# A two-layer graph network on one core: the attention steps of a group moved eleven slots ahead in a written-out plan, one copy behind another reader, two bias copies on another engine

## The chip, the cores and the metric

One Trainium2 chip, one core of it. The metric is the device time of the kernel in microseconds, as the median of several runs. All tensors are float32.

## The reference

128 graphs of 128 nodes with 256 features. Layer 0 is a graph convolution, layer 1 a graph attention with eight heads; both are preceded by a layer norm with a ReLU, and both add their input.

```
h   = relu(layernorm(x));   x1 = x + adj @ (h @ w0) + b0
h2  = relu(layernorm(x1))
feat_proj = (h2 @ fc_w + fc_b) split in 8 heads
logits = q + k^T                          # q, k: one number for each node and head
masked = leaky_relu(logits + (1 - adj) * -1e9, 0.01)
attn   = softmax(masked);   out = attn @ feat_proj
y = sigmoid(concat(out) @ fp_w + fp_b + h2);   result = x1 + y
```

## The kernel before

**Groups and units.** Four graphs make a group, so there are 32 groups, numbered from 0. The main loop has one period for each group. In a period TensorE does the attention products of its group in four units (two halves of the heads, two pairs of heads in each): it aggregates the features with the attention (`aggregate`, line 614) and multiplies the result by the folded weights of the heads (`multiply`, line 661). `take` (line 632) carries each aggregate out of PSUM: five tensors are copied or subtracted on ScalarE, VectorE and GpSimd (f0, f3, f4, f1 are ScalarE copies; f5 = g - f0 is a VectorE subtraction that reads the same PSUM bank as f4; f6 and f2 are GpSimd subtractions). Each aggregate takes one of four PSUM banks in turn, shared with the products of layer 0 and with q and k.

**Slots.** A unit has eleven steps, the list `ORDER`, so a period has 44 slots. In each slot TensorE gets four 128x256 products' worth of work (an `aggregate`, or a `multiply` of the unit before), and then the steps that `PLAN` has for this slot are issued. A plan entry is (slot, who, function, arguments): `who` says which group the step works on, counted from the group of the period (1 is the next group), and "u" means the units themselves. The order of the text is the order on each engine: nothing is rescheduled, each engine and the one DMA queue in use (SyncE's, called SP) runs its own instructions strictly in this order, and waits where an operand is not there.

**What a group goes through before its period.** Layer 0 of group g+3 (`n1_apply`, `first_a`, `first_b`, `n2_stats`) runs in slots 25 to 41 of period g; ScalarE copies `ahT` for `first_a` in slot 35, TensorE needs them for `first_b` in slots 37 and 40. `n2_apply`, `leave_h2` and `fetch_h2` (slots 3 to 5) make h2 of group g+2 and pass it through device memory for a blockwise transpose; `turn_h2_blocks`, `make_qk`, `turn_qk`, `load_k` (slots 18, 24, 28, 34) make q and k of group g+2, k again through device memory (`k_mem`, then `kq`). The attention of group g+1 then fills slots 0 to 33 of period g, graph by graph:

- `masked` (line 523) on VectorE: a transposing spread of `kq` into 128x1024 (L518), and the mask added (L526)
- `leaky` (line 536) on ScalarE: eight instructions, one for a head (L539)
- `head_max` (L547) on VectorE, `exps` on ScalarE (L555), eight for a graph
- `normal` (line 560): a reciprocal on VectorE (L563), and a product on GpSimd (L564)
- `leave_attention` and `fetch_attention` for each pair of graphs: 1 MB to device memory (`a_mem`, L431) and back in four transfers (`attnB`, L575); the second waits for the first in the SP queue
- `turn` (line 586): a blockwise transpose on VectorE (L588), in four parts: pair 0 and 1 of the first half of the heads in slots 34 and 40, pair 0 and 1 of the second half in slots 12 and 13 of the next period

**What follows a period.** `combine` (line 695) of the group before, in slots 6 and 11: ScalarE copies an accumulator with the bias to `p1` (L718), VectorE adds (L704), and the accumulators in PSUM (one set, `acc0` and `acc1`) are free for the new group, which first writes them in slots 12 and 18. Then `leave_z`, `fetch_z`, `turn_z`, `residual` (GpSimd), `sigmoid` (ScalarE, slot 28), `finish` (VectorE, slot 29), `store`. `begin` and `load_blocks` (slot 8) load the inputs of later groups on the same SP queue: `xg`, `ag`, and four transfers `agB`.

Periods 0, 1 and 31 have plans of their own. `EARLIER`, `ATTENTION` and `QK` exist only in the changed kernel.

Of the kernel before, what the change touches and what calls it, by code (L numbers as in the profile page):

```python
# [10 lines left out]
AF = mybir.ActivationFunctionType  # L11
ALU = mybir.AluOpType
# [16 lines left out]
def gnn_then_gat_kernel(  # L29
# [16 lines left out]
    nc = tc.nc  # L46
    NG = x.shape[0] // GB
# [40 lines left out]
    fpb_o = const.tile([P, NC], FP, name="fpb_o")  # L88
# [525 lines left out]
    def aggregate(u, b, c):  # L614
        s = u["s"]
        g = u["g", b, c] = bank([P, HU * P], "g_ps")
        w = HU * P // len(u["pairs"])
        for n, pair in enumerate(u["pairs"]):
            lhsT = (
                s["hs"][:, pair]  # L620
                if c == 2
                else s["h2"][:, 2 * pair + b].rearrange("p j c q -> p (j c q)")[:, ts(c, P)]
            )
            nc.tensor.matmul(  # L624
                g[:, n * w : (n + 1) * w],
                lhsT=lhsT,
                rhs=s["aT", pair, u["half"]][:, b, u["heads"]],
                start=True,
                stop=True,
            )  # L630

    def take(u, b, c):

        g, f = u["g", b, c], u["f"]

        def new(m):
            f[m] = pool["un"].tile([P, HU * P], FP, name=f"f{m}", tag=f"f{m}")
            return f[m]

        if (b, c) == (0, 0):  # L640
            nc.scalar.copy(new(0), g)  # L641
        elif (b, c) == (1, 1):
            nc.scalar.copy(new(3), g)  # L643
        elif (b, c) == (1, 2):
            nc.scalar.copy(new(4), g)  # L645
            nc.vector.tensor_tensor(new(5), g, f[0], ALU.subtract)  # L646
            nc.gpsimd.tensor_tensor(new(6), f[3], f[5], ALU.subtract)  # L647
        else:
            nc.scalar.copy(new(1), g)  # L649
            nc.gpsimd.tensor_tensor(new(2), f[1], f[5], ALU.subtract)  # L650
# [4 lines left out]
    ORDER = [("g", 0, 0), 3, 0, ("g", 1, 1), 1, 4, ("g", 1, 2), 6, 5, ("g", 0, 1), 2]  # L655

    def acc_of(s, part, slots, pairs):
        acc = s["acc", part]
        return acc[:, pairs, slots].rearrange("p a s n -> p s a n") if s["g"] in PAIRWISE else acc[:, slots, pairs]
# [24 lines left out]
    def z_blocks(s, k0, k1, pairs):  # L684

        if s["g"] == NG - 1:
            z = s["zT"].rearrange("p (k a i q) -> p k a i q", k=4, a=2, q=Q)
        else:
            z = s["zT"].rearrange("p (i k a q) -> p k a i q", k=4, a=2, q=Q)
        return z[:, k0:k1, pairs]  # L690

    def blocks(t):
        return t.rearrange("p s a (i q) -> p s a i q", q=Q)

    def combine(u, m):

        s = u["s"]
        pairs = slice(u["pairs"][0], u["pairs"][-1] + 1)  # L700
        n = len(u["pairs"])

        def add(o, a, b):
            nc.vector.tensor_tensor(o, a, b, ALU.add)  # L704

        def acc(part, a, b):
            return acc_of(s, part, slice(a, b), pairs)

        def temp(name, slots):
            return small.tile([P, slots, 2, P], FP, name=name, tag=name, bufs=1)[:, :, 0:n]  # L710

        if m == 4:
            if pairs.start == 0:
                s["zT"] = pool["un"].tile([P, GB * D], FP, name="zT", tag="zT", bufs=1)
            p1 = temp("p1", 2)
            w = s["w"] = temp("w", 2)
            for c in range(NC):
                nc.scalar.activation(  # L718
                    p1[:, c : c + 1], acc(0, 0, 1), AF.Identity, bias=fpb_o[:, c : c + 1]
                )  # L720
            add(w, acc(0, 1, 3), p1)
            add(z_blocks(s, 0, 1, pairs), blocks(acc(0, 3, 4)), blocks(p1[:, 0:1]))
        elif m == 2:
            w = s["w"]
            p6 = temp("p6", 1)
            v = temp("v", 2)
            nc.vector.tensor_copy(p6, acc(1, 0, 1))
            add(v, acc(1, 1, 3), p6.to_broadcast([P, 2, n, P]))
            add(
                z_blocks(s, 2, 4, pairs), blocks(w),  # L730
                blocks(v[:, 0:1]).to_broadcast([P, 2, n, NB, Q]),
            )
            add(z_blocks(s, 1, 2, pairs), blocks(w[:, 1:2]), blocks(v[:, 1:2]))
# [48 lines left out]
    def sigmoid(s, b0, nb):  # L782
        z = s["z"][:, b0 : b0 + nb]
        nc.scalar.activation(z, z, AF.Tanh, scale=0.5)

    def finish(s, b0, nb):
        bs = slice(b0, b0 + nb)
        nc.vector.scalar_tensor_tensor(
            s["z"][:, bs], s["z"][:, bs], 0.5, s["x1"][:, bs], ALU.mult, ALU.add
        )  # L790

    def store(s, b0, nb):
        bs = slice(b0, b0 + nb)
        nc.sync.dma_start(
            out[GB * s["g"] + b0 : GB * s["g"] + b0 + nb].rearrange("b n d -> n b d"),
            s["z"][:, bs],
        )
# [3 lines left out]

    PLAN = [
        (0, "u", take, 0, 0, 0),
        (0, 1, masked, 0),
        (0, 1, masked, 1),
        (0, 1, leaky, 0),
        (3, "u", take, 0, 1, 1),
        (3, 2, n2_apply, 0),
        (3, 2, n2_apply, 1),
        (3, 2, leave_h2),  # L810
# [13 lines left out]
        (13, -1, fetch_z),  # L824
        (11, "u", take, 1, 0, 0),
        (11, 1, leaky, 2),
        (12, 0, turn, 0, 1),
        (12, 1, masked, 3),
        (12, 1, normal, 0),
        (13, 0, turn, 1, 1),  # L830
        (14, "u", take, 1, 1, 1),
        (14, 1, head_max, 2),
        (14, 1, exps, 1, 0, 8),
        (17, "u", take, 1, 1, 2),
        (18, 2, turn_h2_blocks),
        (18, 1, normal, 1),
        (18, 1, leave_attention, 0),
        (20, 1, fetch_attention, 0),
# [6 lines left out]
        (21, -1, residual, 1),  # L845
        (22, "u", take, 2, 0, 0),
        (22, 1, exps, 3, 0, 4),
        (24, 2, make_qk),
        (25, "u", take, 2, 1, 1),
        (25, 1, normal, 2),  # L850
        (25, 1, exps, 3, 4, 4),
        (25, 3, n1_apply, 0),
        (25, 3, n1_apply, 1),
        (27, "u", combine, 1, 4),
        (28, "u", take, 2, 1, 2),
        (28, 2, turn_qk),
        (28, 1, normal, 3),
        (28, 3, turn_blocks),
        (28, 4, n1_stats, 0),
# [28 lines left out]
    FIRST_PLAN = [  # L888
        (0, "u", take, 0, 0, 0),
        (0, 3, load_blocks),  # L890
        (3, "u", take, 0, 1, 1),
        (3, 0, leaky, 3),
        (3, 0, exps, 2, 0, 4),
        (7, "u", take, 0, 1, 2),
        (7, 0, exps, 2, 4, 4),
        (7, 0, head_max, 3),
# [86 lines left out]
    ]  # L983


    SECOND_PLAN = [step for step in PLAN if step != (5, 1, masked, 2)]
    SECOND_PLAN.insert(SECOND_PLAN.index((6, "u", combine, -1, 4)) + 1, (6, 1, masked, 2))
    for old, new in (((12, 0, turn, 0, 1), (12, 0, turn, 1, 0)),):
        SECOND_PLAN[SECOND_PLAN.index(old)] = new
    LAST_PLAN = [step for step in PLAN if step != (12, 0, turn, 0, 1)]  # L990
    LAST_PLAN.insert(LAST_PLAN.index((5, 1, masked, 2)), (4, 0, turn, 0, 1))
    plans = {0: FIRST_PLAN, 1: SECOND_PLAN, NG - 1: LAST_PLAN}

    groups = [{"g": g} for g in range(NG)]
    pool = {}
# [113 lines left out]
    for g in range(NG):  # L1109
        cur = groups[g]  # L1110
        last = units[-1]
        units = []
        for n in range(4):
            each = g in PAIRWISE
            units.append({
                "s": cur,
                "pairs": (n // 2,) if each else (0, 1),
                "half": n % 2 if each else n // 2,
                "heads": slice(0, HU) if each else slice(n % 2 * 2, n % 2 * 2 + 2),
                "first": n % 2 == 0 if each else n == 0,  # L1120
                "last": n % 2 == 1 if each else n == 3,
                "f": {},
            })
        for slot in range(4 * len(ORDER)):
            n, i = divmod(slot, len(ORDER))
            o = ORDER[i]
            if isinstance(o, tuple):
                aggregate(units[n], o[1], o[2])
            elif n or last:
                multiply(units[n - 1] if n else last, o)  # L1130
            for at_, who, f, *args in plans.get(g, PLAN):
                if at_ != slot:
                    continue
                if who == "u":
                    u = last if args[0] < 0 else units[args[0]]
                    if u and not (f is combine and args[0] > 0 and g not in PAIRWISE):
                        f(u, *args[1:])
                elif g + who in range(NG):
                    f(groups[g + who], *args)
            if g == NG - 1 and slot == 33:  # L1140
                turn_z_by_products(cur, 0)
                sigmoid(cur, 0, 2)
            if g == NG - 1 and slot == 35:
                finish(cur, 0, 2)
                store(cur, 0, 2)
# [42 lines left out]
```

## Time and profile before

| what | value |
|---|---|
| median of 3 runs | 1747.33 us (1746.8 to 1747.98) |
| the profiled execution | 1749.97 us, its span 1748.0 us |
| mean granted TensorE clock | 0.96 |
| ScalarE `exps`, 1024 instructions (L555) | 398.6 us busy |
| ScalarE `leaky`, 1024 instructions (L539) | 313.7 us busy |
| VectorE `masked`, spread and add (L518, L526) | 156.9 and 180.6 us busy |
| moved by DMA | 251.34 MB, 144 GB/s |

A row of the profile names the line of the kernel, the engine, the operation and the tiles (out<-in); "idle before, releaser" tells how long the engine sat idle just before such instructions and what it had waited for. The chain of waits is followed back from the last instruction to what released it. The periods can be read off TensorE's rows: the second pair's product of slot 0 waits for `attnT` in nearly every period, for example at 968.82, 1024.02 and, two periods before the last, at 1602.48 us.

### The profile page before, as it was taken

How to read it: one execution, taken by the hardware profiler on the slowest of the kernel's cores; microseconds unless marked ns; L12 is line 12 of the kernel's file. 1: busy time of each engine (PE TensorE's matmuls, PEld its weight loads, DVE VectorE, ACT ScalarE, POOL GpSimd, SP SyncE). 2: the span in 40 equal slices, each digit the busy share in tenths (PEclk: the TensorE clock that was granted, in tenths of full speed). 3: DMA queues.
4: the chain of work that ended last, by engine and by line, in shares of the span. 5: the costliest groups of instructions: out<-in, count | busy, mean ns of one | idle time of the engine just before them, and what ended most of it. 6: DMA issues, size and time to landing. Idle time of an engine off the chain costs nothing.

```text
span 1748.0 us, 24792 instructions
## 1 busy us (share of the span) xinstructions
PE 1539.2 (88%) x7661; PEld 1291.6 (74%) x7661; DVE 1174.1 (67%) x1816; ACT 1194.6 (68%) x4045; POOL 917.4 (52%) x845
## 2 busy tenths in 40 slices
PE   7789898989888899888989888989888998988898
PEld 6567777777777777777777777777777877777686
DVE  6667676667676666676667676667676667675654
ACT  4778766668766668766668766678766678666662
POOL 6646454556454555445555445555445655445453
PEclk9999999999999999999999999999999999999999
DMA  4136555565555465555565545564554565554441
GB/s 162 27 93 184 144 155 136 148 171 156 148 153 152 136 170 156 148 135 156 147 173 146 156 130 144 158 183 137 148 147 139 161 177 144 142 139 130 140 133 48
DMA packets 281760, 251.34 MB, mean 144 GB/s; under 512 B 155398, under 2 KB 237724, under 8 KB 273436
## 3 DMA queue, kind: packets, MB, share of 16 engines
q1 hardware_dynamic: 281628, 249.77, 51.5%
q8 instruction: 60, 0.98, 0.3%
q14 instruction: 72, 0.59, 0.1%
HBM read 135.93 MB, written 113.77 MB: 143 GB/s over the span
## 4 chain that ended last, share of the span: by engine, by line
ACT 47%; DMA 18%; DVE 14%; PE 9%; issue 6%; POOL 5%; SPq 2%; DVEq 0%; POOLq 0%; ACTq 0%
ACT attn L555 17%; ACT attn L539 14%; DMA attnB<-a_mem 9%; DMA a_mem<-attn 7%; ACT h L326 6%; PE acc L676 5%; POOL attn L564 4%; DVE attn L526 3%; DVE attn L518 3%; PE g_ps L624 3%; DVE attnT L588 2%; ACT f L649 2%; ACT f L643 2%; SPq L575 2%; ACT f L645 2%
## 5 line engine op out<-in xcount | busy, mean ns | idle before, releaser
L676 PE MATMUL acc<-f,wts 128*128 128x256 f32 (+1 forms) x3920 | 914.5, 375 | 69.5 <-DVE zT L704 69.5
L676 PEld LDWEIGHTS acc<-f,wts 128*128 128x128 f32 x3920 | 726.2, 199 | 194.3 <-ACT f L649 76.2
L624 PE MATMUL g_ps<-attnT,h 128*128 128x256 f32 (+1 forms) x1464 | 419.9, 405 | 74.6 <-DVE attnT L588 71.9
L555 ACT ACTIVATE attn<-attn,nmax 128x128 f32<-128x128 f32 x1024 | 398.6, 405 | 0.0
L647 POOL TENSOR_TENSOR f<-f,f 128x512 f32<-128x512 f32 x128 | 162.8, 1272 | 407.3 <-DVE f L646 407.3
L624 PEld LDWEIGHTS g_ps<-attnT,h 128*128 128x128 f32 x1464 | 277.1, 196 | 133.7 <-DVE attnT L588 82.0
L539 ACT ACTIVATE attn<-attn,q 128x128 f32<-128x128 f32 x1024 | 313.7, 397 | 85.9 <-DVE attn L526 85.9
L564 POOL TENSOR_TENSOR attn<-attn,total 128x1024 f32<-128x1024 f32 x128 | 249.0, 1946 | 153.2 <-DVE total L563 152.6
L588 DVE STREAM_TRANSPOSE attnT<-attnB 128x1024 f32<-128x1024 f32 x124 | 151.9, 1225 | 170.2 <-DMA attnB<-a_mem 141.0
L646 DVE TENSOR_TENSOR f<-g_ps,f 128x512 f32<-128x512 f32 x128 | 88.1, 688 | 201.9 <-ACT f L645 201.7
L555 ACT ACTIVATION_READ_ACCUMULATOR attn<-attn,nmax 128x1 f32 x1024 | 209.5, 205 | 0.0
L526 DVE TENSOR_TENSOR attn<-attn,mask 128x1024 f32<-128x1024 f32 x128 | 180.6, 1411 | 4.5
L547 DVE TENSOR_REDUCE nmax<-attn 128x8 f32<-128x1024 f32 x128 | 153.9, 1202 | 33.3 <-ACT attn L539 33.2
L650 POOL TENSOR_TENSOR f<-f,f 128x512 f32<-128x512 f32 x128 | 164.7, 1287 | 3.3 <-ACT f L649 3.3
L649 ACT COPY f<-g_ps 128x512 f32<-128x512 f32 x128 | 75.4, 589 | 127.4 <-PE g_ps L624 126.8
L641 ACT COPY f<-g_ps 128x512 f32<-128x512 f32 x128 | 75.1, 587 | 123.0 <-PE g_ps L624 123.0
L518 DVE STREAM_TRANSPOSE attn<-kq 128x1024 f32<-128x1024 f32 x128 | 156.9, 1226 | 2.8 <-DMA kq<-k_mem 2.8
L645 ACT COPY f<-g_ps 128x512 f32<-128x512 f32 x128 | 74.6, 582 | 115.8 <-PE g_ps L624 115.6
L624 PE MATMUL g_ps<-attnT,hs 128*128 128x256 f32 (+1 forms) x488 | 132.5, 392 | 9.0 <-POOL hs L612 9.0
L390 PE MATMUL x_ps<-w_sb,ahT 128*128 128x256 f32 x512 | 120.5, 379 | 0.0
L305 POOL TENSOR_SCALAR rstd<-mv 128x4 f32<-128x4 f32 x61 | 12.7, 225 | 203.8 <-DVE mv L294 203.7
L624 PEld LDWEIGHTS g_ps<-attnT,hs 128*128 128x128 f32 x488 | 92.0, 191 | 22.0 <-POOL hs L612 10.0
(107 smaller groups left out, 1524.3 us busy)
## 6 DMA issues: line engine op xcount, KB each, us to landing
a_mem<-attn SPq DMA_DIRECT2D x62, 1024.0 KB, 3.8
attnB<-a_mem SPq DMA_DIRECT2D x248, 256.0 KB, 4.7
xg<-in_x_dram SPq DMA_DIRECT2D x32, 512.0 KB, 4.2
z_mem<-zT SPq DMA_DIRECT2D x31, 512.0 KB, 2.7
zB<-z_mem SPq DMA_DIRECT2D x124, 128.0 KB, 3.0
out_dram<-z SPq DMA_DIRECT2D x31, 512.0 KB, 4.7
h_mem<-h SPq DMA_DIRECT2D x29, 512.0 KB, 2.8
h2B<-h_mem SPq DMA_DIRECT2D x116, 128.0 KB, 2.9
```

The source lines that it names most:

```text
L390: nc.tensor.matmul(op[:, bb, :], lhsT=s["ahT"][:, 2 * b2 + bb, c, :], rhs=w0_sb[:, c, :], start=(c == 0), stop=(c == NC - 1),)
L518: nc.vector.transpose(s["v", b], s["kq"][:, :, b].unsqueeze(3).to_broadcast([P, NB, H, Q]),)
L526: nc.vector.tensor_tensor(a, a, s["mask"][:, b, :] .rearrange("p (j c) -> p j c", c=Q) .unsqueeze(2) .to_broadcast([P, NB, H, Q]), ALU.add,)
L539: nc.scalar.activation(a[:, :, h, :], a[:, :, h, :], AF.Prelu, bias=s["q"][:, b, h : h + 1], alpha=0.01,)
L547: nc.vector.tensor_reduce(nmax, a.rearrange("p j h c -> p h j c"), AX.XY, ALU.max, negate=True)
L555: nc.scalar.activation(a[:, :, h, :], a[:, :, h, :], AF.Exp, bias=s["nmax", b][:, h : h + 1], accum_out=s["total", b][:, h : h + 1],)
L564: nc.gpsimd.tensor_tensor(a, a, total.unsqueeze(1).unsqueeze(3).to_broadcast([P, NB, H, Q]), ALU.mult)
L588: nc.vector.transpose(attention_tile(s, pair, half).rearrange("p b h (i r) -> p i b h r", r=Q), s["ab", pair][:, :, :, ts(half, HU)],)
L624: nc.tensor.matmul(g[:, n * w : (n + 1) * w], lhsT=lhsT, rhs=s["aT", pair, u["half"]][:, b, u["heads"]], start=True, stop=True,)
L647: nc.gpsimd.tensor_tensor(new(6), f[3], f[5], ALU.subtract)
L650: nc.gpsimd.tensor_tensor(new(2), f[1], f[5], ALU.subtract)
L676: nc.tensor.matmul(acc, lhsT=wt[m][:, u["half"] * HU + h, :], rhs=f[:, n], start=(first and n == 0 and m in ((3, 6) if each else (3, 1, 6, ...
```

## The change

- In `take`, the copy of f4 is issued after the subtraction that makes f5.
- In `combine`, the two copies with the bias (`p1`) go to VectorE.
- In `PLAN`, the two late `turn` entries go from slots 12 and 13 to 2 and 3, and `turn_h2_blocks`, `make_qk` and `turn_qk` go from 18, 24 and 28 to 21, 25 and 29.
- All attention steps and all q and k steps of group 5 and later are then issued eleven slots earlier than `PLAN` says; groups 2, 3 and 4 are 0, 4 and 8 slots earlier. `turn` is not among them. Steps with slots below eleven land in the period before, so slots 33 to 43 of period g now hold the start of the attention of group g+2.
- In each slot, the steps that are not moved are issued first.

```diff
         elif (b, c) == (1, 2):
+            nc.vector.tensor_tensor(new(5), g, f[0], ALU.subtract)
             nc.scalar.copy(new(4), g)
-            nc.vector.tensor_tensor(new(5), g, f[0], ALU.subtract)
...
             for c in range(NC):
-                nc.scalar.activation(
-                    p1[:, c : c + 1], acc(0, 0, 1), AF.Identity, bias=fpb_o[:, c : c + 1]
+                nc.vector.tensor_scalar(
+                    p1[:, c : c + 1], acc(0, 0, 1), fpb_o[:, c : c + 1], None, ALU.add
                 )
...
-        (12, 0, turn, 0, 1),
+        (2, 0, turn, 0, 1),
...
-        (13, 0, turn, 1, 1),
+        (3, 0, turn, 1, 1),
...
-        (18, 2, turn_h2_blocks),
+        (21, 2, turn_h2_blocks),
...
-        (24, 2, make_qk),
+        (25, 2, make_qk),
...
-        (28, 2, turn_qk),
+        (29, 2, turn_qk),
...
+    ATTENTION = (masked, leaky, head_max, exps, normal, leave_attention, fetch_attention)
+    QK = (turn_h2_blocks, make_qk, turn_qk, load_k)
+    EARLIER = {2: 0, 3: 4, 4: 8}
+
+    plans = {g: [] for g in range(NG)}
+    plans[0] = FIRST_PLAN
+    for f_of in (False, True):
+        for g in range(1, NG):
+            for at_, who, f, *args in PLAN:
+                moved = f in ATTENTION or f in QK
+                if moved != f_of:
+                    continue
+                if g == 1 and f is turn and who == 0:
+                    at_ += 10
+                    args = (1, args[0])
+                slot = len(ORDER) * 4 * g + at_
+                if moved:
+                    slot -= EARLIER.get(g + who, 11)
+                period, at_ = divmod(slot, 4 * len(ORDER))
+                who = who if who == "u" else who + g - period
+                plans[period].append((at_, who, f, *args))
```

In a steady period of the changed kernel the SP queue therefore has this order: `leave_h2`, `fetch_h2` (slots 3, 5), `leave_attention` of pair 0 (7), the six loads (8), `fetch_attention` of pair 0 (9), `leave_z`, `fetch_z` (11, 13), `k_mem` (18), `leave_attention` of pair 1 (19), `fetch_attention` of pair 1 (22), the four `kq` (23), `store` (34). Before it was: `leave_h2`, `fetch_h2`, the six loads, `leave_z`, `fetch_z`, pair 0 out (18) and back (20), `k_mem` (28), pair 1 out (30) and back (33), the four `kq` (34), `store`.

More of the change, by code (lines that the diff above doesn't have):

```diff
@@ L983, in gnn_then_gat_kernel @@
     ]
[L986 to L992, printed above, removed]
+    ATTENTION = (masked, leaky, head_max, exps, normal, leave_attention, fetch_attention)
[18 more added lines that the diff above has]
+                plans[period].append((at_, who, f, *args))
     groups = [{"g": g} for g in range(NG)]
@@ L1130, in gnn_then_gat_kernel @@
                 multiply(units[n - 1] if n else last, o)
-            for at_, who, f, *args in plans.get(g, PLAN):
+            for at_, who, f, *args in plans[g]:
                 if at_ != slot:
```

## The prediction

> **What bounds the kernel now.** I read the busy shares first, then the chain of waits, then the waits, the SP queue and TensorE in order of time.
>
> ```profile
> PE 1539.2 (88%) x7661; PEld 1291.6 (74%) x7661; DVE 1174.1 (67%) x1816; ACT 1194.6 (68%) x4045; POOL 917.4 (52%) x845
> ...
> ACT attn L555 17%; ACT attn L539 14%; DMA attnB<-a_mem 9%; DMA a_mem<-attn 7%; ACT h L326 6%; PE acc L676 5%; POOL attn L564 4%; DVE attn L526 3%; DVE attn L518 3%; PE g_ps L624 3%; DVE attnT L588 2%; ACT f L649 2%; ACT f L643 2%; SPq L575 2%; ACT f L645 2%
> ```
>
> No engine is full: TensorE has 88%, but the chain that ends last is the attention of the next group. One turn of it, in order of time (start, duration):
>
> ```profile
> 1007.69 1.93 POOL attn L564
> ...
> 1009.64 5.72 DMA a_mem<-attn
> ...
> 1016.69 5.91 DMA attnB<-a_mem
> ...
> 1022.72 1.25 DVE attnT L588
> 1023.97 0.59 DVE x L397
> ...
> 1025.74 1.25 DVE attn L518
> ```
>
> The last graph's product goes out and back, VectorE turns it (slot 40), and `masked` of the next group (slot 0), behind it in VectorE's queue, starts at once at 1025.74. So the attention is a loop with one turn per period: the spread of graph 0 starts at 970.54 and at 1025.74. TensorE pays for it here:
>
> ```profile
> DVE f L646 <- ACT f L645: 201.7, 65, 6.7
> DVE attnT L588 <- DMA attnB<-a_mem: 141.0, 27, 9.9
> PE g_ps L624 <- DVE attnT L588: 71.9, 30, 7.3
> PE acc L676 <- DVE zT L704: 69.5, 29, 3.2
> ...
> 546.91 0.70 PE L624 MATMUL g_ps<-attnT,h 128*128 128x256 f32 x2 [2.19 <-DVE attnT L588]
> 547.45 3.52 PE L676 MATMUL acc<-f,wts 128*128 128x256 f32 x8
> ```
>
> After such a wait eight products take 3.52 us, not the usual 1.89; the granted clock at 548 to 550 is 0.50. Counting TensorE's rows at full clock (0.864 us a slot, 1.9 for `first_a`, 3.5 for `first_b`, 0.7 for q and k) gives 44.0 us a period; slot 0 of periods 2 and 30 (179.81 and 1653.26) lie 28 turns of 52.6 us apart. The 8.6 us between are these waits and the slow clock after them.
>
> SP has one period like this:
>
> ```profile
> 820.28 0.38 SPq L435 DMA_DIRECT2D h_mem<-h  x1
> ...
> 825.12 0.42 SPq L67 DMA_DIRECT2D xg<-in_x_dram  x1
> ...
> 829.95 0.48 SPq L431 DMA_DIRECT2D z_mem<-zT  x1
> 833.75 1.74 SPq L742 DMA_DIRECT2D zB<-z_mem  x4
> ...
> 850.62 0.34 SPq L431 DMA_DIRECT2D a_mem<-attn  x1
> 854.43 1.74 SPq L575 DMA_DIRECT2D attnB<-a_mem  x4
> 856.27 1.80 SPq L498 DMA_DIRECT2D kq<-k_mem  x4
> ...
> kq<-k_mem SPq DMA_DIRECT2D x128, 16.0 KB, 4.6
> ```
>
> The loads hold SP 4.8 us (825.12 to 829.95), `zB` waits 3.8 us for `z_mem`, `attnB` 3.8 us for `a_mem`, and `kq` stands behind `attnB`.
>
> **What the change removes.** `attnB` comes back far ahead of `turn` in slots 34 and 40, so those waits go (71.9 us on TensorE, most of the slow clock after them). The moved `p1` takes two ScalarE copies, 0.8 us, off the path to `acc0` and puts 0.8 us on VectorE (as L727, 413 ns each). VectorE (36.1 us busy of some 52.4 in windows of a period) and ScalarE (36.7) have room. If nothing else held, a period would be 44 us plus a few small waits.
>
> **What it adds: a new loop.** Slots 33 to 43 now hold `masked`, `leaky`, `head_max` of a group among the last steps of layer 0, and in each queue they stand ahead of these: `leaky` 0 (slot 33) before the `ahT` copies (35) on ScalarE, `finish` before `masked` on VectorE, and `kq` (23) behind pair 1's way out and back on SP. Let 0 be the start of `masked` of graph 0. By rows of before (net spacing when back to back):
> - to the start of `leaky` 0: 2.54 (1025.74 to 1028.28); `leaky` 2.36; first `ahT` copy 0.5: 5.4
> - `first_b`, eight products, which wait for that copy: 1.73 at full clock, 3.2 at half (1654.27, after a wait of 7.3). TensorE will have waited long, so 3.2: 8.6
> - VectorE, strictly in this order: add 0.7, statistics 1.15, `head_max` 0 1.13, `masked` 2 2.45, f5 of slot 39 0.6: 14.6
> - ScalarE: f4 now waits for that f5 (before, f5 waited for f4), and all the rest stands behind it: f4, f1 0.47 each, `exps` 0 3.09, f0 0.47, `leaky` 2 2.36, f3 0.47, `n2_apply` 1.98, `exps` 1 3.09: 27.0
> - VectorE over the same stretch: turn, add, statistics, two maxima, `masked` 3, two turns, `combine` with `p1`, f5 of slot 7: 12.4 too, 27.0
> - GpSimd: f6 1.25, `normal` 1 1.9: 30.2
>
> Now SP may send pair 0 out: 0.35; the six loads, which pass from ahead of it to behind it, 4.9 (4.6 to 5.2 before); pair 0 back 1.75 (the outward way ends meanwhile); `z_mem` to `zB`, 3.7 to 4.8 before, now behind 1 MB of `attnB`: I take 4.9; `zB` 1.75; `k_mem` 0.35; pair 1 out, waited for 3.8; then pair 1 back and `kq`, whose last issue is 3.3 us after the first `attnB` and lands 4.6 later: 7.9. Sum 25.7. `normal` 3 would be ready earlier than SP (at about 40 against 44), so SP sets it. The next `masked` 0 can start at 55.9: **the loop takes 56 us, not 52.6**, and TensorE, with about 47 of work and small waits, idles some 8 us before each `first_b`.
>
> Bounds. The front part is 28.7 if `first_b` runs at full clock, 30.7 if the adds are slowed like the one of 1.96 us at 974.24. `z_mem` behind `attnB` has no row; nearest are a store behind nothing (2.7 to landing) and `out_dram`, a store of the same size that follows `attnB` and `kq` closely (4.0 to 6.2, median 4.7), plus 0.5 to issue; I lean to the second, as its place is alike. `a_mem` takes 3.8, at times 5.7. `kq` lands in 3.8 to 5.9. All the lowest at once give SP 23.4, all the highest 31.0; with one or two of them at their ends it is 24.4 to 28.5, and the loop 53 to 59.
>
> Here the Trainium skill bears, in "DMA: Bandwidth & Descriptors", section "Queues, rings and completion order": each DMA engine takes the descriptors of a queue in ring order. Our two medians for a store (2.7 and 4.7 us) agree. By the rule `z_mem` always pays for `attnB`; without it the loop would be some 2 us shorter.
>
> "TensorE: Matmul & The Clock Gate", section "What's actually happening", says that the clock falls to half after an idle window of about 3.4 us; here a wait of 2.19 was enough once (546.91), and by either an idle of 8 us is paid.
>
> **Sum.** `masked` 0 of group 5 starts at 287.7 before; the ramp can gain up to 15 us, I take 4. There follow 26 turns to group 31. From there 15.6 us to slot 0 of period 30, about 40.5 for period 30 (no layer 0, no q and k left, 50.7 before), and 44.1 from 1703.93 to the end as before: 100. Without the loads the last two turns save 6. Total 378 + 26 x 56 = 1834 against a span of 1748.0. That execution was 2.6 us above the median of runs, its span 0.7 above it; so **1835 us**. Break-even is a loop of 52.7.
>
> **Rivals.**
> - *Faster.* The place is SP, the price of `kq`. If SP reaches pair 1's way out before `normal` 3 is done, the loop is closed by ScalarE alone: about 38.5 to the end of `normal` 3 at full clock (39.1 before), 3.8 out, 7.9 for `kq`, 50.2. Total 378 + 26 x 50.2 = 1683, 65 us faster. It decides from the point where SP's 25.7 falls below 22.4. For it: SP has free stretches before, such as 858.6 to 871.9. Against: all my lowest terms at once give 23.4. If `kq` were early as well, TensorE would set about 47.6, 1616 us. 17%.
> - *No change.* The parts of SP overlap better than I count, and the loop is 52.5 to 52.8. For it: all the lowest bounds, 28.7 and 23.4, give 52.1. Against: they would have to be met nearly all at once, though TensorE's idle time excludes the full clock. 4%.
> - *Much slower.* The 1 MB transfers of pair 0, the loads, `z_mem` and pair 1 are now one burst; if `a_mem` takes 5.7 and `z_mem` 6.5 in each turn, the loop is 59.5, 1925 us. 10%.
> - *Does not do what it says.* f4 behind f5 is free only while VectorE is on time. In slot 39 it is some 5 us late, so ScalarE idles there. Undone, f1 would still wait for TensorE's slot 42 at about 13 to 15, so this is worth 1 us of a turn, 26 us in all, and does not turn the sign.
>
> **How the numbers follow.** The forecast (loop 53.5 to 58.5, 1770 to 1900 us) has 69%, faster 17%, no change 4%, over 1900 us 10%. About 0.2% (3.5 us) is what a measurement can tell. The range of 8 in 10 reaches from 1700, into the faster case, to 1905. Faster 0.17, same 0.04, slower 0.79.
>
> **What would show it.** Right: spreads of graph 0 (L518) 56 us apart; before each an idle VectorE released by `kq<-k_mem`; TensorE waiting for the `ahT` copy 6 to 10 us before `first_b` (L390), clock 0.5 behind it; hardly any wait of `turn` for `attnB`. Wrong: the spread waits for nothing or for `finish`; `kq` issued within 40 us of the spread before; TensorE's waits under 4 us a period. It would be wrong as a whole if SP's stretch from pair 0 out to `kq` is shorter than 22 us.

## The result, and the profile after

The changed kernel takes **1993.22 us** (median of 4 runs, 1992.11 to 2002.91), the kernel before 1747.65 us beside it (4 runs, 1746.8 to 1753.78): 1.1409 times as long, interval 1.1364 to 1.1453. The profiled execution has a span of 1990.4 us and a mean granted clock of 0.90 (0.96 before). It is slower, as forecast, but by 246 us and not by 88, and outside the range of 1700 to 1905 us.

Three lines of its page: the busy shares, the chain that ended last by line, and the landing time of the store `z_mem`, which was 2.7 us before.

```profile
PE 1603.2 (81%) x7661; PEld 1344.7 (68%) x7661; DVE 1169.9 (59%) x1886; ACT 1173.7 (59%) x3975; POOL 940.8 (47%) x845
...
DMA z_mem<-zT 9%; PE acc L676 8%; DMA a_mem<-attn 7%; PE x_ps L390 7%; DMA kq<-k_mem 6%; ACT attn L539 6%; ACT attn L555 6%; SPq L575 4%; PE g_ps L624 4%; DVE attn L518 3%; SPq L77 3%; DVE attn L526 3%; SPq L742 2%; ACT h L326 2%; DVE nmax L547 2%
...
z_mem<-zT SPq DMA_DIRECT2D x31, 512.0 KB, 6.5
```

Before, `exps` and `leaky` on ScalarE led the chain (17% and 14%); both are now at 6%. `z_mem` leads with 9% and `kq` has 6%, and neither is on the line of before; with `a_mem` (7% in both) these are transfers of the SP queue. Between them stand TensorE's products L676 and L390 (`first_b`), with 8% and 7%. Every engine is less busy in share.

One turn of the loop in the changed kernel's timeline (start, duration, and in brackets the idle time before):

```profile
1018.37 1.25 DVE L518 STREAM_TRANSPOSE attn<-kq 128x1024 f32<-128x1024 f32 x1 [3.96 <-DMA kq<-k_mem]
...
1080.62 1.25 DVE L518 STREAM_TRANSPOSE attn<-kq 128x1024 f32<-128x1024 f32 x1 [3.95 <-DMA kq<-k_mem]
...
1085.51 1.04 ACT L381 COPY ahT<-ah_ps 128x512 f32<-128x512 f32 x2
...
1086.12 3.74 PE L390 MATMUL x_ps<-w_sb,ahT 128*128 128x256 f32 x8 [8.19 <-ACT ahT L381]
```

The spread of graph 0 waits for `kq` each time, 62.25 us apart here and 62.0 on the mean of 23 turns (337.36 to 1764.19 us). Behind it come `leaky`, the `ahT` copies, and a TensorE that has stood for 8.19 us and does eight products in 3.74.

SP in the same turn:

```profile
1049.42 0.34 SPq L431 DMA_DIRECT2D a_mem<-attn  x1
...
1056.22 2.88 SPq L575 DMA_DIRECT2D attnB<-a_mem  x4
1059.20 0.38 SPq L431 DMA_DIRECT2D z_mem<-zT  x1
1065.86 1.73 SPq L742 DMA_DIRECT2D zB<-z_mem  x4
1067.68 0.38 SPq L493 DMA_DIRECT2D k_mem<-k  x1
1068.15 0.38 SPq L431 DMA_DIRECT2D a_mem<-attn  x1
1072.40 1.74 SPq L575 DMA_DIRECT2D attnB<-a_mem  x4
1074.24 3.00 SPq L498 DMA_DIRECT2D kq<-k_mem  x4
```

This is the predicted order, from pair 0 out to `kq`, and each step takes longer than the forecast had it: 31.2 us from 1049.42 to the next spread (29.7 to 32.1 in the turns between 337.36 and 1639.89 us). The view by stretches of time (length, busy time of each engine, then granted clock, mean busy share of the 16 DMA engines, and GB/s) for the front part and the two parts of SP's stretch:

```profile
1018.37:1049.42 31.05, 24.23 (x100) 20.36 (x100) 24.24 (x33) 21.78 (x77) 12.26 (x15) 0.84 0.12 32
1049.42:1068.15 18.73, 15.74 (x80) 13.48 (x81) 5.96 (x12) 11.65 (x43) 7.48 (x5) 0.91 0.86 218
1068.15:1080.62 12.47, 8.66 (x47) 7.21 (x45) 5.64 (x13) 2.60 (x4) 9.09 (x8) 1.00 0.86 233
```

In the first half of a turn the DMA engines do almost nothing (0.12, 32 GB/s, 1.0 MB), in the second they are busy at 0.86 and move 7.0 MB (218 x 18.73 + 233 x 12.47). VectorE and ScalarE stand the other way round: 24.24 and 21.78 us of work in the first half, 11.60 and 14.25 in the second. The change has made two halves of a turn out of what ran side by side.

The waits say the same (who waited for what: us in total, times, longest):

```profile
DVE z L749 <- DMA zB<-z_mem: 294.1, 30, 11.8
...
PE x_ps L390 <- ACT ahT L381: 205.1, 27, 8.4
...
DVE attn L518 <- DMA kq<-k_mem: 104.7, 28, 4.3
```

VectorE's wait for `attnB`, 141.0 us before, is down to 5.0.

### The profile page after: what moved, and what is told of

It is laid out like the page before. It is cut to its first block, busy times and chain, and to the rows that moved or that the text cites. A ratio compares the mean times of both kernels' runs of the same rounds, so it can differ in the third digit from the quotient of the medians.

```text
span 1990.4 us, 24642 instructions
## 1 busy us (share of the span) xinstructions
PE 1603.2 (81%) x7661; PEld 1344.7 (68%) x7661; DVE 1169.9 (59%) x1886; ACT 1173.7 (59%) x3975; POOL 940.8 (47%) x845
## 4 chain that ended last, share of the span: by engine, by line
DMA 26%; PE 19%; ACT 17%; DVE 16%; SPq 14%; issue 5%; POOL 3%; DVEq 0%; ACTq 0%; POOLq 0%
DMA z_mem<-zT 9%; PE acc L676 8%; DMA a_mem<-attn 7%; PE x_ps L390 7%; DMA kq<-k_mem 6%; ACT attn L539 6%; ACT attn L555 6%; SPq L575 4%; PE g_ps L624 4%; DVE attn L518 3%; SPq L77 3%; DVE attn L526 3%; SPq L742 2%; ACT h L326 2%; DVE nmax L547 2%
## 5 line engine op out<-in xcount | busy, mean ns | idle before, releaser
L676 PE MATMUL acc<-f,wts 128*128 128x256 f32 (+1 forms) x3920 | 935.9, 380 | 17.0 <-ACT attn L555 7.3
L676 PEld LDWEIGHTS acc<-f,wts 128*128 128x128 f32 x3920 | 734.5, 201 | 150.8 <-ACT attn L555 19.9
L647 POOL TENSOR_TENSOR f<-f,f 128x512 f32<-128x512 f32 x128 | 163.8, 1280 | 558.4 <-DVE f L645 459.9
L624 PE MATMUL g_ps<-attnT,h 128*128 128x256 f32 (+1 forms) x1464 | 401.4, 394 | 22.2 <-ACT f L649 12.8
L390 PE MATMUL x_ps<-w_sb,ahT 128*128 128x256 f32 x512 | 169.4, 490 | 205.1 <-ACT ahT L381 205.1
L646 ACT COPY f<-g_ps 128x512 f32<-128x512 f32 x128 | 74.5, 582 | 377.1 <-DVE f L645 376.9
L390 PEld LDWEIGHTS x_ps<-w_sb,ahT 128*128 128x128 f32 x512 | 123.7, 249 | 238.2 <-ACT ahT L381 216.4
L749 DVE STREAM_TRANSPOSE z<-zB 128x1024 f32<-128x1024 f32 x31 | 38.6, 1246 | 300.7 <-DMA zB<-z_mem 294.1
L778 POOL TENSOR_TENSOR z<-z,h 128x256 f32<-128x256 f32 x124 | 86.3, 728 | 211.1 <-DVE z L749 211.1
L526 DVE TENSOR_TENSOR attn<-attn,mask 128x1024 f32<-128x1024 f32 x128 | 163.8, 1280 | 4.5
L624 PE MATMUL g_ps<-attnT,hs 128*128 128x256 f32 (+1 forms) x488 | 143.8, 418 | 9.9 <-POOL hs L612 9.9
L645 DVE TENSOR_TENSOR f<-g_ps,f 128x512 f32<-128x512 f32 x128 | 86.7, 678 | 101.1 <-PE g_ps L624 100.6
L624 PEld LDWEIGHTS g_ps<-attnT,hs 128*128 128x128 f32 x488 | 103.8, 215 | 28.8 <-POOL hs L612 10.9
```

What stands on the lines that cost most here:

```text
L390: nc.tensor.matmul(op[:, bb, :], lhsT=s["ahT"][:, 2 * b2 + bb, c, :], rhs=w0_sb[:, c, :], start=(c == 0), stop=(c == NC - 1),)
L526: nc.vector.tensor_tensor(a, a, s["mask"][:, b, :] .rearrange("p (j c) -> p j c", c=Q) .unsqueeze(2) .to_broadcast([P, NB, H, Q]), ALU.add,)
L624: nc.tensor.matmul(g[:, n * w : (n + 1) * w], lhsT=lhsT, rhs=s["aT", pair, u["half"]][:, b, u["heads"]], start=True, stop=True,)
L676: nc.tensor.matmul(acc, lhsT=wt[m][:, u["half"] * HU + h, :], rhs=f[:, n], start=(first and n == 0 and m in ((3, 6) if each else (3, 1, 6, ...
```

## The experiments

Times are medians; the kernel before ran beside them and took 1752.9 to 1755.1 us. The ratio is to it.

| run | us | ratio | interval |
|---|---|---|---|
| e5_small: before, with both small edits | 1682.10 | 0.9585 | 0.9551 to 0.9620 |
| e9_f4first: before, with f4 behind f5 | 1702.88 | 0.9716 | 0.9702 to 0.9730 |
| e10_p1: before, with the bias copies on VectorE | 1732.09 | 0.9880 | 0.9859 to 0.9901 |
| e11_move: the move alone | 2077.17 | 1.1849 | 1.1831 to 1.1867 |
| e3_f4: changed, f4 ahead of f5 again | 2044.80 | 1.1657 | 1.1622 to 1.1693 |
| e1_loads: changed, loads earlier | 1914.85 | 1.0900 | 1.0870 to 1.0929 |
| e2_kq: changed, `kq` earlier | 1923.02 | 1.0951 | 1.0932 to 1.0970 |
| e4_leaky: changed, `leaky` 0 behind `ahT` | 1913.41 | 1.0906 | 1.0884 to 1.0927 |
| e6_all3: changed, these three together | 1763.50 | 1.0051 | 1.0027 to 1.0075 |
| e8_z: changed, `z_mem` ahead of pair 0 back | 1994.95 | 1.1382 | 1.1350 to 1.1414 |
| e7_five: moved five slots, not eleven | 1747.24 | 0.9955 | 0.9936 to 0.9973 |
| e12_masked0: e5_small, with `masked` 0 and `kq` earlier | 1688.53 | 0.9630 | 0.9616 to 0.9645 |
| e13_kqwait: the same, another place for `kq` | 1599.79 | 0.9129 | 0.9105 to 0.9154 |
| e14_leaky0: and `leaky` 0 earlier | 1597.81 | 0.9117 | 0.9096 to 0.9138 |

**The parts of the change.** The diff has three parts, and four runs take them apart. The first two are the two hunks of the diff alone, applied to the kernel before.

```diff
 # e9_f4first
-            nc.scalar.copy(new(4), g)
             nc.vector.tensor_tensor(new(5), g, f[0], ALU.subtract)
+            nc.scalar.copy(new(4), g)
 # e10_p1
-                nc.scalar.activation(
-                    p1[:, c : c + 1], acc(0, 0, 1), AF.Identity, bias=fpb_o[:, c : c + 1]
+                nc.vector.tensor_scalar(
+                    p1[:, c : c + 1], acc(0, 0, 1), fpb_o[:, c : c + 1], None, ALU.add
```

> The kernel before, with only the two small edits: f4 behind f5, and p1 on VectorE. No step is moved. Theory A (the loop): the small edits are no part of the loss; ScalarE loses two copies (0.8 us) out of the loop M0 to normal 3, and f5 no longer waits for a late f4; 0 to 2 us a period, 1690 to 1755. Theory D (f4 behind a late f5 holds ScalarE, which is the chain that ends last): 1 to 3 us a period slower, 1780 to 1840.

> The kernel before, with nothing of the change but f4 behind f5. Both small edits together took 73 us. Theory A: most of it is this swap, because f5 of slots 7, 17 and 28 no longer waits on VectorE for a ScalarE copy that stands behind exps (201.7 us of VectorE waits in the kernel before), so that masked and head_max come earlier: 1690 to 1715 us where the kernel before takes 1755. Theory B: f4's place is worth nothing by itself, as VectorE has room, and the bias copies carry the gain: 1745 to 1755 us.

> The kernel before, with nothing of the change but the two bias copies of a period on VectorE. Theory A (f4's place carries most): ScalarE is 0.8 us shorter in each of 31 periods, 25 us at most, 1730 to 1755 us. Theory B (the bias copies carry the gain, by freeing acc0 earlier): 1680 to 1700 us.

The two together gain 4.15% (73 us, 8 more than the best that was expected), the swap of f4 alone 2.84%, the bias copies alone 1.20%; the parts nearly add up to the whole. The wait of VectorE's f5 for ScalarE's f4, 201.7 us in the kernel before, is what the swap removes; in its place ScalarE waits for f5 (208.0 us in e9_f4first).

e11_move is the changed kernel without both hunks:

> The changed kernel without both small edits, so the move of the attention and of q and k alone. Theory A: the small edits are worth about as much here as in the kernel before, 50 us for f4 (2045 without it) and some 10 to 30 for the bias copies: 2050 to 2080 us. Rival: the bias copies cost something once they stand on VectorE in the front part of the new loop, where VectorE's and ScalarE's chains are equally long: 2015 to 2040 us.

The move alone is 18.5% slower, so the small edits are worth 4.4 points of the time before there too, and the move costs 18 points (about 320 us) whether they are made or not. All the loss is the move's. e3_f4 undoes only the swap in the changed kernel:

```diff
-            nc.vector.tensor_tensor(new(5), g, f[0], ALU.subtract)
             nc.scalar.copy(new(4), g)
+            nc.vector.tensor_tensor(new(5), g, f[0], ALU.subtract)
```

> The changed kernel, with the copy of f4 ahead of f5 again. Theory A (the loop): ScalarE no longer waits for f5 in slot 39 (7.7 us at most, 376.9 us in all), but VectorE's own order gives the same front part of the loop (31 us to f5 of slot 7), so the time stays within 10 us of 1993. Theory D (the small edits cost the time: ScalarE stands still behind a late VectorE): the 377 us of waiting come back at least by a third, 1860 or less.

Both expectations failed: it costs 2.5 points more of the time before. A piece of its chain of waits, at the end of the front part:

```profile
1074.75 2.69 ACT attn L555 x14
1077.44 0.48 ACT f L645
...
1078.01 0.70 DVE f L646
...
1080.01 1.92 POOL attn L564
```

L645 is f4 here, L646 f5. f4 stands behind the `exps` of graph 1 on ScalarE, f5 waits for it on VectorE, f6 and `normal` 1 on GpSimd come behind f5, and pair 0 goes out behind these. The turns are 63.8 us, 1.8 longer.

**Three steps of the loop, one at a time, then together.** Each edit takes one thing out of the predicted chain of the changed kernel: the six loads between pair 0 out and back, `kq` behind pair 1, and `leaky` 0 ahead of the `ahT` copies.

```diff
 # e1_loads
                     slot -= EARLIER.get(g + who, 11)
+                if f in (begin, load_blocks) and g > 1:
+                    slot -= 11
 # e2_kq
+        (29, 2, load_k),
...
-        (34, 2, load_k),
 # e4_leaky
-        (0, 1, leaky, 0),
+        (2, 1, leaky, 0),
```

> The changed kernel, with the six loads of slot 8 issued eleven slots earlier too (slot 41 of the period before), so that they no longer stand between pair 0's way out and its way back in the SP queue. Theory A (the period is a loop that runs through the SP queue, 62.3 us a turn): SP's stretch from pair 0 out to pair 0 back falls from 6.8 us to the 3.8 to 4.4 of a_mem alone, the four attnB issue in 1.8 instead of 2.9, z_mem to zB takes about 5.5 instead of 6.6; the turn becomes 57 to 58 us and the time 1870 to 1890. Theory B (the burst of traffic costs, whatever its order): the same bytes move, the turn stays within 1 us, 1970 to 1995. Theory C (ScalarE and VectorE order alone, the ahT copies behind leaky): no change, 1985 to 1995.

> The changed kernel, with load_k right behind k_mem in the SP queue, ahead of pair 1's way out and back. Theory A (the loop closes through kq): kq lands some 5 us sooner, the spread of graph 0 no longer waits for it (104.7 us of waiting in all, 3.95 in a turn) but starts right behind finish, which stands at the end of the path z_mem, zB, turn_z, residual, sigmoid; the turn becomes about 58.3, the time 1885 to 1900. Theory B (kq and the z path are both held by the same burst, so an earlier kq only shifts the burst): less than 1.5 us a turn, 1955 to 1990. Theory C (VectorE and ScalarE order): no change, 1985 to 1995.

> The changed kernel, with leaky of graph 0 two slots later, so that in slot 35 the ahT copies stand ahead of it on ScalarE. Theory A (the loop): TensorE no longer waits for ahT (205 us in all, 7 to 8 in a turn) and first_b runs at full clock, but the loop only loses VectorE's wait for first_b (3.3 us in a turn): the turn becomes 58.5 to 60, the time 1900 to 1930. Theory C (TensorE's wait for ahT and its half clock behind it are the loss themselves): 8 to 10 us a turn come back, 1730 to 1790.

> The changed kernel with three edits at once: loads eleven slots earlier, load_k right behind k_mem, leaky of graph 0 behind the ahT copies. Theory A (one loop, several places): the savings add where they lie in a row; the loop is then closed by z_mem, zB, turn_z, residual, sigmoid, finish, about 52 us a turn, and the time 1720 to 1780. Theory B (the places run side by side, each hides the next): no better than the best single edit by more than 30 us, 1870 or more.

Singly they gain 5.1, 4.6 and 5.0 points of the time before (89, 80 and 88 us), together 13.6 (238 us): each lies on the path, and they nearly add. That is the loop as predicted, since a step beside the path would have gained nothing. The gain of e4_leaky is in the range that theory A gave, and so is the time of the three together; the other two gains fell short of what was expected. In e1_loads pair 0 comes back 4.1 us after it goes out (6.8 with the loads between), but `z_mem` still needs 6.05 us to `zB` (1014.65 to 1020.70) with no load near it:

```profile
1012.31 2.24 SPq L575 DMA_DIRECT2D attnB<-a_mem  x4
1014.65 0.38 SPq L431 DMA_DIRECT2D z_mem<-zT  x1
1020.70 1.73 SPq L742 DMA_DIRECT2D zB<-z_mem  x4
```

That points to the 1 MB of `attnB` ahead of it, and not to the loads; e8_z below tries it. In e2_kq the spread waits for `kq` no longer but for VectorE, where it stands behind `finish`, which follows `zB` by way of `turn_z`, `residual` and `sigmoid` (VectorE waits 11.76 us for `zB` there, and the turn is 59.4 us). In e4_leaky TensorE waits most for `attnT` in place of `ahT`, 142.1 us in all.

With all three mended the kernel still takes 1763.50 us, 81 more than with the small edits alone. What these consist of wasn't taken apart; its SP now waits 365.6 us for the add that frees the buffer of `xg`, and VectorE 207.7 us for `zB`.

**Is it the place of `z_mem`?** e8_z puts the way back of pair 0 behind `zB`.

```diff
-        (20, 1, fetch_attention, 0),
+        (25, 1, fetch_attention, 0),
```

> The changed kernel, with fetch_attention of pair 0 five slots later, so that SP issues z_mem and zB ahead of the four attnB of pair 0; everything else in place. Theory A1 (z_mem is slow because its 512 KB stand behind 1 MB of attnB in the queues): z_mem to zB falls from 6.6 us to 3.7 to 4.8 as before the change, attnB issue in 1.8 instead of 2.9, pair 1's way out may pay up to 2 us of it back; the turn of 62.3 us becomes 58.5 to 60, the time 1900 to 1945. Theory B1 (z_mem is slow because of the loads ahead of it, which still stand there): z_mem to zB stays above 6 us and the time within 1.5%, 1965 to 2005.

SP in this run:

```profile
1060.23 0.50 SPq L431 DMA_DIRECT2D z_mem<-zT  x1
1064.92 1.73 SPq L742 DMA_DIRECT2D zB<-z_mem  x4
...
1069.12 0.38 SPq L431 DMA_DIRECT2D a_mem<-attn  x1
1076.52 1.74 SPq L575 DMA_DIRECT2D attnB<-a_mem  x4
```

`zB` now follows `z_mem` by 4.69 us, not 6.66, though the loads still stand ahead of it: so it was `attnB`, as theory A1 said. But `attnB` of pair 0 is then in flight when pair 1 goes out, and `a_mem` takes 7.40 us, not 4.25. The time is the same, as theory B1 said: 2.0 us are gained at `z_mem` and 1.0 at the issues of `attnB` (1.85 us, 1066.70 to 1068.55, not 2.88), and 3.2 are given back, with the DMA engines at 0.93 and 260 GB/s in those 7.40 us. The other turns from 350 to 1500 us are alike (medians: `z_mem` to `zB` 3.7 us and not 6.6, `a_mem` of pair 1 8.2 and not 4.3). This new order within the burst moves the waiting and doesn't shorten it.

**A shorter move.** e7_five moves the attention and q and k by 5 slots (the ramp by 0, 2, 4), leaves the late `turn` entries in slots 12 and 13, and has `load_k` right behind `k_mem`. The two lines that set the shift:

```diff
-    EARLIER = {2: 0, 3: 4, 4: 8}
+    EARLIER = {2: 0, 3: 2, 4: 4}
...
-                    slot -= EARLIER.get(g + who, 11)
+                    slot -= EARLIER.get(g + who, 5)
```

> The changed kernel with a shift of 5 slots and not 11 (2 and 4 for groups 3 and 4), turn of the second half of the heads left in slots 12 and 13 as before, and load_k right behind k_mem. masked of graph 0 then stands in slot 39, behind the ahT copies and the first half of layer 0 but ahead of turn of pair 1 (slot 40), pair 0 leaves behind fetch_z in the SP queue as before. Theory A: no loop is left that is longer than TensorE's work: turn finds attnB there, kq is early; 46 to 49 us a period, 1590 to 1670. Rival (moving the attention ahead at all puts its VectorE work into layer 0's slots and makes TensorE wait there): 52 us or more, 1750 to 1850.

1747.24 us is as slow as the kernel before within half a per cent, and 65 us slower than the small edits alone: far from theory A, and at the edge of the rival's range. A shorter move is no help in itself; which wait holds it wasn't taken apart.

**One step moved.** Where VectorE stands idle for `attnB` in e5_small (3.75 us before 1036.44), there is room for `masked` 0 (2.5 us) of the group after. e12_masked0 moves only this step, and `load_k` with it; e13_kqwait differs from e12_masked0 in the place of `load_k` alone; e14_leaky0 moves `leaky` 0 as well.

```diff
 # e12_masked0, against e5_small
-        (0, 1, masked, 0),
+        (29, 2, load_k),
-        (34, 2, load_k),
+        (38, 2, masked, 0),
 # e13_kqwait, against e12_masked0
-        (29, 2, load_k),
+        (32, 2, load_k),
 # e14_leaky0, against e13_kqwait
-        (0, 1, leaky, 0),
+        (41, 2, leaky, 0),
```

> The kernel before with both small edits, and of the whole move one step alone: masked of graph 0 goes from slot 0 into slot 38 of the period before, into the 3.75 us that VectorE waits there for attnB, and load_k goes to slot 29, behind k_mem and ahead of pair 1's way out. Theory A: the loop with one turn a period is still closed by the attention, and its part on VectorE ahead of leaky 0 is 2.5 us shorter: 1600 to 1660 us, against 1682 for the small edits alone. Rival: something else closes the loop by now (TensorE's own 47 us, the product behind the last turn, or kq ahead of pair 1 delaying a_mem): 1670 to 1720 us.

SP in e12_masked0, and then in e13_kqwait:

```profile
1021.91 1.73 SPq L575 DMA_DIRECT2D attnB<-a_mem  x4
1023.74 0.38 SPq L493 DMA_DIRECT2D k_mem<-k  x1
1029.96 1.73 SPq L498 DMA_DIRECT2D kq<-k_mem  x4
1031.79 0.38 SPq L431 DMA_DIRECT2D a_mem<-attn  x1
```

```profile
1014.06 0.38 SPq L493 DMA_DIRECT2D k_mem<-k  x1
1018.55 0.34 SPq L431 DMA_DIRECT2D a_mem<-attn  x1
1019.41 2.63 SPq L498 DMA_DIRECT2D kq<-k_mem  x4
1023.03 1.73 SPq L575 DMA_DIRECT2D attnB<-a_mem  x4
```

In the first, `kq` waits 6.2 us for a store of 16 KB that lies behind the 1 MB of `attnB`, and pair 1 stands in the queue behind it. `masked` 0 is early, and nothing is gained (0.9630 against 0.9585 for the small edits alone). In the second, pair 1 goes out first, and `kq` is issued while SP would wait for `a_mem` anyway.

> As the run before it (both small edits, masked of graph 0 in slot 38 of the period before), but load_k in slot 32: behind pair 1's way out and ahead of its way back, where SP waits 3.8 us for a_mem anyway. Theory A: the run before it gained nothing because kq, queued ahead of pair 1, waited 6.2 us for k_mem to land behind the 1 MB of attnB of pair 0 and held pair 1's way out by some 4 us; with that gone, the 2.5 us of masked 0 come through: 1600 to 1655 us. Rival: the place of kq is worth nothing, another loop (TensorE's products with the maxima and copies they wait for) sets about 50 us a period: 1675 to 1695 us.

> As the run before it, with leaky of graph 0 in slot 41 of the period before as well, so that neither masked 0 nor leaky 0 stands behind the last turn. Theory A (the attention still closes the loop): another 1 to 3 us of a period, 1540 to 1625 us, TensorE's own 47 us a period being the floor. Rival: leaky 0 now stands ahead of the copies of slots 42 and 0 on ScalarE and holds TensorE, as leaky 0 did ahead of ahT in the changed kernel: no better than the run before it, or up to 40 us slower.

e13_kqwait takes 1599.79 us: 8.7% less than the kernel before and 89 us less than e12_masked0, by one entry's place in the queue. e14_leaky0 gains nothing that can be told from it; TensorE is at 93% in e13_kqwait. So the same step moved ahead gains 4.6 points over the small edits or nothing, by what its transfer meets on SP. `load_k` in slot 32 with `masked` 0 left in slot 0, and that place of `kq` within the eleven-slot move, weren't tried; that the transfers alone make the whole move slow is therefore not shown, and the 81 us that e6_all3 keeps are open.

## Why the prediction was right and wrong

**Right: the loop and what closes it.** What was named as a sign of it is there, but for the 56 us between spreads: the spread released by `kq`, TensorE standing 8.19 us before `first_b` with the slow clock behind it, no wait of `turn` for `attnB` to speak of. e1_loads, e2_kq and e4_leaky show that three of its steps are on the path. The front part, 30.2 us by rows of before, took 31.05. The parts around the 26 turns are off by 9 and 14 us, and that their sum came out near is luck, as they err in opposite ways: the first turn starts at 274.9 us (283.7 forecast), and 107.6 us follow the last spread at 1882.8 (94 forecast). The last step from 1834 to 1835 us has its sign wrong, as taking 0.7 off gives 1833; nothing hangs on it.

**Wrong: the size of SP's terms.** This is the step that failed, and it is nearly the whole miss: 26 turns of 61.8 us (274.9 to 1882.8) instead of 56 make 152 of the 156 us between the two spans, 1834 and 1990.

| SP's stretch | forecast us | measured us |
|---|---|---|
| pair 0 out | 0.35 | 0.44 |
| six loads | 4.9 | 6.36 |
| pair 0 back | 1.75 | 2.98 |
| `z_mem` to `zB` | 4.9 | 6.66 |
| `zB` and `k_mem` | 2.1 | 2.29 |
| pair 1 out | 3.8 | 4.25 |
| pair 1 back, `kq` to its landing | 7.9 | 8.22 |
| sum | 25.7 | 31.2 |

Every term is above its forecast, and the sum is at the bound "all the highest at once" (31.0). The forecast took each term from a row in which the rest of the burst wasn't there, and let them err independently ("with one or two of them at their ends"). They are not independent: 7.0 MB go through the engines in one stretch, at 218 to 233 GB/s, and the engines are busy for 0.86 of it. e8_z shows that what one transfer gains another gives back. Before, a full stretch (the six loads) ran at 251 GB/s:

```profile
825.12:829.95 4.83, 4.83 (x19) 4.07 (x18) 4.76 (x7) 4.83 (x21) 2.42 (x2) 0.76 1.07 251
```

At that rate 7.0 MB are 27.9 us, already 2 us above the forecast. The other 3 us are where the engines stand idle though SP is in the middle of its list. The view of the transfers from 1049.4 to 1068.2 in 40 equal slices of 0.47 us (busy share in tenths) shows one such place:

```profile
DMA  8499999985999999998999979999898100000578
```

From 1064.4 to 1066.8 hardly a byte moves: `z_mem` is through, and `zB`, which SP issues when it has landed (1065.86), hasn't begun. The same happens between the way out of pair 1 and its way back, from 1071.6 to some 1073.5. So an estimate from rows of the trace, bytes over the rate of a full stretch and 4 to 5 us for the two idle places, gives about 32 us where 31.2 were measured. The rival "much slower" came nearest, at 59.5 us a turn and 10%. Its `z_mem` of 6.5 us is what was measured (6.66), its `a_mem` of 5.7 is not (4.25), and the slower loads and issues of `attnB` (1.5 and 1.2 us more) had a price in no rival.

**Wrong in sign: f4.** The forecast said that to undo f4 behind f5 would be worth 1 us of a turn. It costs 1.8 (e3_f4). The argument looked at the f4 of slot 39 alone; the one that decides stands behind `exps` 1, at the end of the front part, where GpSimd waits for f5. And the swap counted as no gain on the time before, where e9_f4first gives 50 us: the 201.7 us of waits that it removes stood in the first of the lines on waits, but no term was worked out from them.

**Right: the bias copies**, 0.8 us a period off ScalarE's path: e10_p1 gains 21 us, 0.7 a period.

**The Trainium skill.** Ring order in "DMA: Bandwidth & Descriptors", section "Queues, rings and completion order", agrees with what was tried: `z_mem` needs 6.7 us behind `attnB` and 4.7 ahead of it (e8_z), and the 16 KB of `k` need 6.2 behind it (e12_masked0) and 2.7 behind `zB` (e2_kq). No run separates the order from the rate that the transfers share. What the forecast drew from it, that the loop would be 2 us shorter without that wait, does not come out: in e8_z the wait moved on to `a_mem`.

The slow clock after an idle TensorE showed in each turn: after 7.6 to 8.4 us without work (342.86 to 1769.84 us) the eight products of `first_b` took 3.4 to 3.8 us, and not the 1.89 that most of them take in the kernel before, and the granted clock of the front part shown is 0.84. The forecast's "enough once" for a wait of 2.19 us is too few: in the kernel before, a wait of 1.96 us (1076.45) was followed by 3.2 us at 0.50 too, while one of 2.18 (599.22) was followed by the full clock.

## What to carry to other kernels

When a plan moves several transfers of one queue next to each other, cost them as one stretch: bytes over the rate that a full stretch of the trace shows, and the idle time wherever the queue waits for a store before it fetches it back; not as a sum of single rows, each taken without the others beside it. Before moving a step, look at what its inputs queue behind: one load of 64 KB was worth 89 us by its place among the stores and fetches of 1 MB, and the best of the two places tried was where the queue would wait anyway. And where two engines read one bank in turn, let the one go first that doesn't stand behind a long block: this alone was worth 2.8%.

## What the hardware showed besides

- Issuing itself takes longer in the burst: the four issues of `attnB` took 1.74 us in the median before and 2.88 behind the loads, the four of `agB` 4.70 where the median before is 3.9 and, with the loads away from pair 0 (e1_loads), 3.1.
- A store of 16 KB (`k_mem`) held the queue for 6.2 us when 1 MB of fetches lay ahead of it (e12_masked0), and for 2.7 us behind `zB` (e2_kq); its size said nothing of its price.
- VectorE's mask add (L526), 128 times the same instruction, took 1411 ns on the mean in the kernel before, 1280 in the changed one and 1541 in e2_kq. As the instruction is the same, the cause should be something beside it; what it is wasn't settled.
